# Seven block products in place of eight for the second product of a graph layer, with two re-ordered stretches

## The chip, the cores and the metric

The kernel runs on one core of a Trainium2 chip. The core has five engines, each of which works through its own instructions in order: TensorE (matrix products, "PE" in the profile, its weight loads are "PEld"), VectorE ("DVE"), ScalarE ("ACT"), GpSimd ("POOL") and SyncE ("SP", which issues transfers). They wait for one another through semaphores. SBUF is the on-chip memory, and PSUM the eight banks that TensorE writes its products to. The metric is the device time of one execution in microseconds (us), smaller is better.

All arithmetic is float32. A matmul instruction in float32 leaves two records in the trace, so "x16" beside a product means eight instructions.

## The reference, cut to what matters

Four graph layers, each added to its input (`x = x + layer(relu(layernorm(x)))`). The input has 128 x 64 x 256 elements, and the kernel works on it in 16 chunks of 512 tokens. The change touches layer 0 and the beginning of the last stretch, in which layers 2 and 3 run together.

```python
# layer 0 (h = relu(layernorm(x)), A_hat = normalised adjacency)
agg = einsum('nm,bmd->bnd', A_hat, h).reshape(-1, 256)
h1  = relu(batchnorm(agg @ W1.T + b1))      # 256 -> 512 channels, statistics over all 8192 tokens
out = batchnorm(h1 @ W2.T + b2)             # 512 -> 256 channels: "the second product"
# layer 2: attention with q, k, v and an output projection
# layer 3: attention with four heads; q and k by seven block products already
```

The batch normalisation needs all tokens before the first value can be used. So the first product runs for all chunks (keeping `z1`, 512 channels, in SBUF), then its statistics are put together, then the second product runs for all chunks.

## The kernel before

The second product of a chunk: four ReLU instructions on ScalarE write `h1`, eight matmuls (four channel blocks `k` for each of two output blocks `m`) fill two PSUM banks, and VectorE takes statistics and copies with the bias. The line numbers are those that the profile names.

```python
    def product2(chunks, by_block):
        h1 = {c: l0b.tile([P, KH, CH], F32, tag="h1", ...) for c in chunks}     # two buffers
        banks = {(c, m): bank(f"z2_{c}_{m}") for c in chunks for m in range(KD)}
        for k in range(KH):
            for c in chunks:
                nc.scalar.activation(h1[c][:, k, :], z1[c][k], AF.Relu, ...)             # L360
        ...
            nc.tensor.matmul(banks[c, m], w2_sb[:, k, ...], h1[c][:, k, :], ...)         # L364
        for c in chunks:
            for m in range(KD):
                nc.vector.bn_stats(st2[:, m, c, :], banks[c, m])                         # L368
                nc.vector.tensor_scalar(z2[c][:, m, :], banks[c, m], bn2_sb[...], ...)   # L369
    # [...]
    product2([0, 1], True)            # the first two chunks, block by block
    # [...]
        for c in range(2, NCH):       # NCH = 16
            if c == NCH - 2:
                weight_transposes()
            if wanted:
                weight_sums(*wanted.pop(0))     # 12 sets for layer 1: 2 loads, 4 GpSimd sums (L483), 2 stores
            product2([c], False)
        sc2, sh2 = bn_params(st2, bn2_sb, const, "bn2", False)
```

In this stretch only TensorE's order is given by hand (`manual_schedule(engines={PE})`); the order on the other engines comes out of the framework's scheduler when the kernel is built. `weight_sums` has two buffers, so a set's loads wait for the stores of the set before the last one.

The opening, by hand on all engines: adjacency, layer normalisation of chunk 0 in two halves (`a00`, `a01`), normalised adjacency, then chunk 1.

```python
        dinv = degrees(setup, others)
        keep_busy(34, "a")                                   # transposes that only keep TensorE at work
        stats = [ln_stats(xts[0], "a00", parts[0])]
        nc.vector.tensor_add(an, adj_bd, ident)
        normalized(setup, an, dinv)                          # rows, transpose (PE), ahat_t from PSUM
        keep_busy(10, "b")
        stats.append(ln_stats(xts[0], "a01", parts[1]))
        for i in range(2):
            ln_apply(hs[0], xts[0], *stats[i], f"a0{i}", parts[i])
        mv, rstd = ln_stats(xts[1], "a1")
        aggregate0(0)
        ln_apply(hs[1], xts[1], mv, rstd, "a1")
        keep_busy(8, "c")
```

Layers 2 and 3 are pipelined over the chunks: a round is a string of steps, `q2+0` being step `q2` for the round's chunk, `exp3-3` step `exp3` for the chunk three before. The first round (chunk 3) follows a filling sequence FIRST, and was the common round with its first two steps swapped:

```python
    FIRST = """... v3a+0 load3+1 v3b+0 apply3+2 square3+2"""          # end of the filling
        run(FIRST, 0)
        ring_places()                                                  # four GpSimd sums of weights (L1276)
        run(ROUND.replace("exp3-3 q2+0 copyq2+0", "q2+0 copyq2+0 exp3-3"), SUP + 1)
        for c in range(SUP + 2, NCH - SUP - 1):
            run(ROUND, c)
    # apply3: four ReLU on ScalarE (L174); square3: four transposes on VectorE (L259)
    # q2: a product on PE (L1108), half copied by ScalarE (L1169); copyq2: the other half by VectorE (L1174)
    # score2: products of q2 and the input (L1191)
```

Of the kernel before, what the change touches and what calls it, by code (L numbers as in the profile page):

```python
# [13 lines left out]
P = 128  # L14
# [5 lines left out]
def kernel(  # L20
# [65 lines left out]
    def bank(name, tag="ps"):  # L86
        return psum[0][0].tile([P, CH], F32, tag=tag, name=name, bufs=psum[0][1][tag])
# [39 lines left out]
    def normalized(setup, an, dinv):  # L127
        rows = setup.tile([P, P], F32, name="rows")
        nc.vector.tensor_scalar(rows, an, dinv, None, op0=OP.mult)
        pt = bank("pt_ahat")  # L130
        nc.tensor.transpose(pt[:, :P], rows, ident)
        nc.vector.tensor_scalar(ahat_t, pt[:, :P], dinv, None, op0=OP.mult)

# [20 lines left out]
    def ln_stats(src, name, tiles=range(NJ)):  # L154
        n = len(tiles)
        st = small.tile([P, n, 6], F32, tag=f"ln_st{n}", name=f"st_{name}")
        mv = small.tile([P, n, 2], F32, tag=f"ln_mv{n}", name=f"mv_{name}")
        for i, j in enumerate(tiles):
            nc.vector.bn_stats(st[:, i, :], src[:, j, :])
            nc.vector.bn_aggr(mv[:, i, :], st[:, i, :])  # L160
        rstd = small.tile([P, n], F32, tag=f"ln_rstd{n}", name=f"rstd_{name}")
        rsqrt(rstd, mv[:, :, 1], EPS)
        return mv, rstd

    def ln_apply(dst, src, mv, rstd, name, tiles=range(NJ), by_pool=False):
# [107 lines left out]
    def bn_params(stats, bn, pool, name, biased):  # L273
# [15 lines left out]
        return sc, sh  # L289


    GATES = (0, 2, 3, 1)
# [21 lines left out]

    z1, hs, aggs = {}, {}, {}

# [19 lines left out]
    def product1(c):  # L336
# [4 lines left out]
        for m in range(KH):  # L341
# [8 lines left out]
            nc.vector.bn_stats(st1[:, m, c, :], z1[c][m])  # L350
        z2[c] = lo

    def product2(chunks, by_block):
# [12 lines left out]
        for c in chunks:  # L366
            for m in range(KD):
                nc.vector.bn_stats(st2[:, m, c, :], banks[c, m])  # L368
                nc.vector.tensor_scalar(z2[c][:, m, :], banks[c, m], bn2_sb[:, 0, m : m + 1], None,  # L369
                                        op0=OP.add)  # L370

    with tc.manual_schedule(engines={mybir.EngineType.PE, mybir.EngineType.DVE,
# [18 lines left out]

        parts = [range(2 * i, 2 * i + 2) for i in range(2)]
        stats = [ln_stats(xts[0], "a00", parts[0])]
        an = setup.tile([P, P], F32, name="an")
        nc.vector.tensor_add(an, adj_bd, ident)
        normalized(setup, an, dinv)
        keep_busy(10, "b")
        stats.append(ln_stats(xts[0], "a01", parts[1]))  # L400
        for i in range(2):
            ln_apply(hs[0], xts[0], *stats[i], f"a0{i}", parts[i])
        mv, rstd = ln_stats(xts[1], "a1")
        aggregate0(0)
        ln_apply(hs[1], xts[1], mv, rstd, "a1")
        keep_busy(8, "c")
# [4 lines left out]
    with tc.manual_schedule(engines={mybir.EngineType.PE}):  # L411
# [4 lines left out]
        w2_sb = l0b.tile([P, KH, D], F32, name="w2_sb", bufs=1)  # L416
        nc.gpsimd.dma_start(w2_sb, w2t.rearrange("(k p) f -> p k f", p=P))
        for c in range(1, NCH):
            if c + 1 < NCH:
                aggregate0(c + 1)  # L420
            if c + 2 < NCH:
                norm0(c + 2)
            product1(c)
# [19 lines left out]

        def weight_transposes():
            for f in range(3 * KD):
                ps = bank(f"wt_{f}")
# [42 lines left out]
        wanted = [(p, q) for p in range(2, SKIP + 1) for q in GATES]  # L489
        for c in range(2, NCH):  # L490
            if c == NCH - 2:
                weight_transposes()
            if wanted:
                weight_sums(*wanted.pop(0))
            product2([c], False)
        sc2, sh2 = bn_params(st2, bn2_sb, const, "bn2", False)
        c2_ps = weight_products()
# [171 lines left out]
    BLOCKS = {1: (0, 8), 2: (2, 9), 3: (7, 14), 4: (3, 10), 5: (4, 11), 6: (5, 12), 7: (6, 13)}  # L669

    def differences(engine, dst, b11, b12, b21, b22):

        t1, t2, t3, t4 = dst
        return [lambda: engine.tensor_tensor(t1, b12, b11, OP.subtract),
                lambda: (engine.tensor_tensor(t3, b22, b12, OP.subtract),
                         engine.tensor_tensor(t2, b22, t1, OP.subtract)),
                lambda: engine.tensor_tensor(t4, b21, t2, OP.subtract)]

# [825 lines left out]
    def store(c, t):  # L1504
# [3 lines left out]
        for r in range(2):  # L1508
# [7 lines left out]
               v3a-2 qd-2 apply3+0 out3-3 score3-2 store-3 square3+0 v3b-2"""  # L1516

    NORM = """exp3-3 q2+0 copyq2+0 sum3-3 load3-1 sums_h-2 v2a+0 divide3-3 score2+0 exp2+0 v2b+0 norm2+1
              divide2+0 turn3-3 qa-2 turn2+0 q5-2 c11-2 out2+0 keep+0 norm3a+0 qb-2 apply2+1 back-2 qc-2
# [8 lines left out]
               norm3+1 pair1+15 pair1+15 q31+0 k31+0 apply3+1 out2+2 keep+2 square3+1 score3+0 norm3+2  # L1528
               v3a+0 load3+1 v3b+0 apply3+2 square3+2"""
    LAST = """exp3-2 sum3-2 load3+0 divide3-2 qa-1 q5-1 c11-1 v3a-1 qb-1 c12-1 qc-1 turn3-2 out3-2 qd-1  # L1530
# [10 lines left out]
    with tc.manual_schedule(engines={mybir.EngineType.PE, mybir.EngineType.DVE,  # L1541
# [6 lines left out]
        ring_places()  # L1548
        run(ROUND.replace("exp3-3 q2+0 copyq2+0", "q2+0 copyq2+0 exp3-3"), SUP + 1)
        for c in range(SUP + 2, NCH - SUP - 1):  # L1550
# [55 lines left out]
```

## Time and profile before

The median of three runs is 1924.26 us (1924.07 to 1924.88). The profile's span is cut here into stretches. Busy times are those of the answer that gives each engine's busy time in given stretches.

| stretch, us | what | PE busy | DVE | ACT | POOL |
|---|---|---|---|---|---|
| 0 to 25.5 | opening | 20.77 | 12.21 | 11.34 | 8.51 |
| 25.5 to 145.9 | layer 0, first product | 120.34 | 71.50 | 73.34 | 22.99 |
| 145.9 to 257.1 | layer 0, second product | 111.20 | 49.77 | 46.79 | 36.69 |
| 257.1 to 1560 | start of layer 1, layer 1 | 1295.65 | 773.34 | 668.61 | 240.42 |
| 1560 to 1588.8 | filling of layers 2 and 3 | 28.10 | 18.91 | 10.85 | 3.75 |
| 1588.8 to 1617.5 | first round | 25.60 | 16.86 | 11.91 | 10.61 |
| 1617.5 to 1924.8 | the other rounds, end | 300.23 | 215.78 | 135.54 | 90.04 |

How to read it: where PE is busy for the whole stretch, only fewer or shorter products help, provided that the other engines still keep up; where it is not, something else ends the wait. The granted clock of TensorE is given with each stretch: it is 1.00 in all of them but the opening (0.93) and the first round (0.88).

### The profile page before, as it was taken

Reading aid. Unit: us, or ns where it says so; the run is one execution under the profiler, and the core shown is the slowest. Engines: PE = TensorE matmul, PEld = TensorE weight load, DVE = VectorE, ACT = ScalarE, POOL = GpSimd, SP = SyncE. Lnnn points to the kernel's source line nnn. Section 1 sums busy time; section 2 is a strip of 40 time slices with the busy share of each in tenths; the row PEclk is TensorE's granted clock in tenths of the full one; section 3 lists DMA queues with packets and bytes.
Section 4 is the critical chain, followed back from the end, with each engine's and each line's share of the span. In section 5 each row is a group of like instructions: output and inputs, shape, how many; then the busy total and the mean of one; then the engine's idle time right before and its main releaser. Section 6 shows DMA issues by size and latency. Waiting matters only on the chain.

```text
span 1924.8 us, 38314 instructions
## 1 busy us (share of the span) xinstructions
PE 1901.9 (99%) x14979; PEld 1463.0 (76%) x14979; DVE 1158.4 (60%) x3019; ACT 958.4 (50%) x2132; POOL 413.0 (21%) x613
## 2 busy tenths in 40 slices
PE   9999999999999999999999999999999999999998
PEld 5444455897897889699689789879969967777776
DVE  6644354556557656755755665665555566677776
ACT  5655434445456455455545545545554543444453
POOL 3204210211211121121121121112112113233232
PEclk9999999999999999999999999999999999999999
DMA  4115711224524521532542452252144244445433
GB/s 130 64 42 211 279 60 66 83 83 160 159 83 141 186 97 64 174 105 93 189 141 83 159 181 83 96 190 103 56 150 128 90 143 142 134 133 154 143 111 111
DMA packets 110499, 240.35 MB, mean 125 GB/s; under 512 B 11376, under 2 KB 74352, under 8 KB 110320
## 3 DMA queue, kind: packets, MB, share of 16 engines
q1 hardware_dynamic: 109568, 236.57, 37.0%
q8 instruction: 118, 1.93, 0.4%
q0 software_dynamic: 320, 1.05, 0.2%
q14 instruction: 61, 0.50, 0.1%
q10 hardware_dynamic: 432, 0.30, 0.0%
HBM read 169.98 MB, written 67.90 MB: 124 GB/s over the span
## 4 chain that ended last, share of the span: by engine, by line
PE 94%; DVE 3%; ACT 1%; DMA 1%; issue 1%; POOL 0%; SPq 0%; DVEq 0%; ACTq 0%; POOLq 0%
PE x L829 22%; PE g L793 18%; PE z L829 11%; PE z L347 6%; PE y L829 6%; PE z L364 6%; PE v L1101 5%; PE p_q L1108 3%; PE u L574 3%; PE v L560 3%; PE X L1297 3%; PE Y L1297 1%; PE agg_a L201 1%; PE agg_c L201 1%; PE s L1191 1%; PE agg_b L201 1%
## 5 line engine op out<-in xcount | busy, mean ns | idle before, releaser
L838 DVE TENSOR_TENSOR gates<-gates,x 128x128 f32<-128x128 f32 (+2 forms) x384 | 119.4, 322 | 334.9 <-PE x L829 327.9
L829 PE MATMUL x<-xd,wset 128*128 128x128 f32 (+2 forms) x1280 | 285.2, 311 | 0.4 <-DVE gates L838 0.2
L829 PE MATMUL x<-hd,wset 128*128 128x128 f32 (+2 forms) x1152 | 246.7, 303 | 0.0
L829 PEld LDWEIGHTS x<-xd,wset 128*128 128x128 f32 x1280 | 202.1, 190 | 17.7 <-DVE gates L838 3.9
L887 POOL TENSOR_TENSOR gates<-gates 128x512 f32<-128x512 f32 (+2 forms) x48 | 74.9, 1559 | 648.1 <-ACT gates L721 648.1
L721 ACT ACTIVATE gates<-gates,bias 128x256 f32<-128x256 f32 (+4 forms) x384 | 170.4, 491 | 67.0 <-DVE gates L838 64.2
L829 PEld LDWEIGHTS x<-hd,wset 128*128 128x128 f32 x1152 | 185.1, 191 | 5.0
L772 ACT ACTIVATE gates<-g,bias 128x512 f32<-128x512 f32 (+2 forms) x240 | 138.0, 609 | 98.1 <-PE g L793 94.7
L793 PE MATMUL g<-hT,wset 128*128 128x256 f32 (+2 forms) x744 | 184.4, 405 | 1.1 <-DVE hT L732 1.1
L793 PEld LDWEIGHTS g<-hT,wset 128*128 128x128 f32 x744 | 140.5, 190 | 44.1 <-issue 8.8
L793 PE MATMUL g<-hT,wih 128*128 128x512 f32 x384 | 166.4, 592 | 0.0
L835 ACT COPY gates<-y 128x128 f32<-128x128 f32 (+2 forms) x192 | 54.1, 293 | 205.4 <-PE y L829 205.0
L829 PE MATMUL z<-hs,wset 128*128 128x128 f32 (+2 forms) x768 | 154.1, 303 | 0.0
L793 PEld LDWEIGHTS g<-hT,wih 128*128 128x128 f32 x384 | 72.3, 190 | 87.7 <-issue 83.2
L829 PEld LDWEIGHTS z<-hs,wset 128*128 128x128 f32 x768 | 119.8, 191 | 3.3
L347 PE MATMUL z<-agg,w_sb 128*128 128x512 f32 x256 | 114.5, 600 | 0.0
L778 DVE TENSOR_TENSOR cell<-gates 128x512 f32<-128x512 f32 (+2 forms) x80 | 50.3, 646 | 101.3 <-ACT gates L772 101.2
L364 PE MATMUL z<-h,w_sb 128*128 128x512 f32 x256 | 110.2, 592 | 0.0
L838 DVE TENSOR_TENSOR gates<-gates,z 128x128 f32<-128x128 f32 (+2 forms) x384 | 104.6, 316 | 0.1
L835 ACT COPY gates<-x 128x128 f32<-128x128 f32 (+2 forms) x192 | 56.5, 295 | 93.9 <-PE x L829 93.1
L721 ACT ACTIVATE gates<-x,bias 128x128 f32<-128x128 f32 (+2 forms) x192 | 74.7, 389 | 50.9 <-PE x L829 48.0
L829 PE MATMUL z<-hT,wset 128*128 128x128 f32 (+1 forms) x512 | 96.9, 301 | 0.0
(243 smaller groups left out, 3644.2 us busy)
## 6 DMA issues: line engine op xcount, KB each, us to landing
wset<-wfar SPq DMA_DIRECT2D x96, 960.0 KB, 6.4
hT<-far_h SPq DMA_DIRECT2D x124, 128.0 KB, 2.9
far_h<-hm SPq DMA_DIRECT2D x16, 512.0 KB, 3.8
far_n<-xs SPq DMA_DIRECT2D x16, 512.0 KB, 7.2
xs<-far_n SPq DMA_DIRECT2D x64, 128.0 KB, 3.1
far_x<-xs SPq DMA_DIRECT2D x16, 512.0 KB, 3.0
x<-far_x SPq DMA_DIRECT2D x64, 128.0 KB, 3.2
xt<-in_x_dram SPq DMA_DIRECT2D x15, 512.0 KB, 4.0
```

The lines of the kernel that those rows point to most:

```text
L201: nc.tensor.matmul(banks[e][half(i), k, j, :], src[half(e), j, f], mat[half(e), half(e)], start=True, stop=True)
L347: nc.tensor.matmul(ps, w1_sb[:, k, m * P : (m + 1) * P], agg[:, k, :], start=(k == 0), stop=(k == KD - 1))
L364: nc.tensor.matmul(banks[c, m], w2_sb[:, k, m * P : (m + 1) * P], h1[c][:, k, :], start=(k == 0), stop=(k == KH - 1))
L721: nc.scalar.activation(gate(q, c, part), src, AF.Tanh if q == 2 else AF.Sigmoid, bias=bs[:, q * KD + c : q * KD + c + 1])
L772: nc.scalar.activation(columns_of(gate(q, c)), natural(banks[q, c][:, :n].rearrange("p (w b) -> p w b", b=nb)), AF.Tanh if q == 2 else AF. ...
L793: nc.tensor.matmul(banks[q, c][:, :n].rearrange("p (w b) -> p w b", b=nb)[:, w, :], block(q, c, k), hv[:, k, w.start * p : (w.stop - 1) * ...
L829: nc.tensor.matmul(folded(self.psum(kind)), wsets[p, self.q][:, BLOCKS[kind][i], :], (ox[self.s] if part == "x" else oh)[kind], start=firs ...
L835: nc.scalar.copy(gate(self.q, kind // 5, halves[kind // 5]), self.psum(kind))
L838: nc.vector.tensor_add(gate(self.q, *dst), gate(self.q, *a), self.psum(kind))
L887: nc.gpsimd.tensor_mul(gates[:, 0, :, :n], gates[:, 0, :, :n], gates[:, 2, :, :n])
L1101: nc.tensor.matmul(ps[:, i, :], hT[:, k, j, :], w[:, k, first : first + D], start=(k == 0), stop=(k == KD - 1))
L1297: nc.tensor.matmul(st[c, tag][:, i * CH // 2 : (i + 1) * CH // 2].rearrange("p (a n) -> p a n", n=P), w, st[c, "o7"][kind], start=first an ...
```

## The change

Three parts.

1. For chunks 2 to 14 the second product is done by seven block products in place of eight (Winograd's form of Strassen's scheme). The 512 input channels are two blocks of rows, the 512 tokens two halves, the 256 output channels two blocks. Sums of weight blocks are made once on GpSimd, sums of data blocks on VectorE, and one of four (`t3`) on GpSimd. Seven products of 2 x (128 x 256) collect in three half-filled PSUM banks X, Y and Z; ScalarE copies four quarters, VectorE adds three. The ReLU is done in place in `z1`, and the result goes back into `z1` too. The products P7 and P4 of a chunk stand among those of the next one, so that TensorE has work while an add or a copy is under way.
2. The opening's order on VectorE is changed: the statistics of the second half of chunk 0 go between other steps, `ahat_t` is taken from PSUM later, and chunk 1's statistics are split in two.
3. The first round gets an order of its own (THIRD): `apply3` and `square3` of chunk 2 move from the end of FIRST to behind `copyq2` and `exp2`, `score2` to ahead of GpSimd's sums, and a `v3a` is brought forward.

The statistics of the second product are now taken from the copied values in SBUF (with the bias), not from PSUM.

```diff
-                nc.vector.bn_stats(st2[:, m, c, :], banks[c, m])
                 nc.vector.tensor_scalar(z2[c][:, m, :], banks[c, m], bn2_sb[...], None, op0=OP.add)
+                nc.vector.bn_stats(st2[:, m, c, :], z2[c][:, m, :])
+    def seven2(c):
+        for k in range(KH):
+            nc.scalar.activation(z1[c][k], z1[c][k], AF.Relu, ...)                # in place
+        b = {(k, j): a[:, :, halves[j]] for k, a in enumerate(z1whole[c]) for j in range(2)}
+        t = l0b.tile([P, 4, KH // 2, CH // 2], F32, tag="h1", name=f"t2_{c}")     # two buffers
+        for f in differences(nc.vector, t, ..., nc.gpsimd): f()     # t1, t2, t4 VectorE, t3 GpSimd
+        at = {1: b[0, 0], 2: b[1, 0], 3: b[1, 1], 4: t[3], 5: t[0], 6: t[1], 7: t[2]}
         # [...] product(kind, bank): two matmuls 128 x 256 that add to the bank
+        product(2, "Z")
+        yield
+        product(1, "X"); copy(0, 0, "X")
+        yield
+        product(5, "Y"); copy(1, 1, "Y"); add(0, 0, "Z")
+        yield
+        product(6, "X"); copy(0, 1, "X")
+        yield
+        product(3, "Y"); add(0, 1, "Y"); bn_stats(... 0 ...)
+        yield
+        product(7, "X"); add(1, 1, "X")
+        yield
+        product(4, "X"); copy(1, 0, "X"); bn_stats(... 1 ...)
+        yield
         # [...] opening
+        late = ln_moments(xts[0], "a01", parts[1])
+        next(late)
         nc.vector.tensor_add(an, adj_bd, ident)
-        normalized(setup, an, dinv)
-        keep_busy(10, "b")
-        stats.append(ln_stats(xts[0], "a01", parts[1]))
+        pt = normalized(setup, an, dinv)
+        keep_busy(12, "b")
+        next(late)
+        stats.append(next(late))
+        ln_apply(hs[0], xts[0], *stats[0], "a00", parts[0])
+        nc.vector.tensor_scalar(ahat_t, pt[:, :P], dinv, None, op0=OP.mult)
+        ln_apply(hs[0], xts[0], *stats[1], "a01", parts[1])
         # [...] the loop of the second product
-        for c in range(2, NCH):
+        last = iter(())
+        for c in range(2, NCH - 1):
             if wanted:
                 weight_sums(*wanted.pop(0))
-            product2([c], False)
+            kinds = seven2(c)
+            for turn in (kinds, last, kinds, kinds, last, kinds, kinds):
+                next(turn, None)
+            last = kinds
+        weight_transposes(range(2)); next(last)
+        weight_transposes(range(2, 3 * KD)); next(last)
+        product2([NCH - 1], False)
         # [...] layers 2 and 3
+    THIRD = """q2+0 copyq2+0 apply3-1 exp3-3 load2+1 v2a+0 score2+0 exp2+0 square3-1 sum3-3 load3-1 sums_h-2
+               v2b+0 divide3-3 divide2+0 qa-2 v3a-2 turn3-3 turn2+0 q5-2 c11-2 out2+0 keep+0 norm3a+0 qb-2
+               back-2 qc-2 norm3b+0 c12-2 qd-2 apply3+0 out3-3 score3-2 store-3 square3+0 v3b-2"""
-               v3a+0 load3+1 v3b+0 apply3+2 square3+2"""
+               v3a+0 load3+1 v3b+0"""
-        run(ROUND.replace("exp3-3 q2+0 copyq2+0", "q2+0 copyq2+0 exp3-3"), SUP + 1)
+        run(THIRD, SUP + 1)
```

In the order of TensorE, one chunk `c` of the new loop is thus P2(c), P7(c-1), P1(c), P5(c), P4(c-1), P6(c), P3(c).

## The prediction

> **What bounds the kernel now.** I read the page's chain first, then the chain in order of time, then the timeline of the three stretches that change.
>
> ```profile
> PE 94%; DVE 3%; ACT 1%; DMA 1%; issue 1%; POOL 0%; SPq 0%; DVEq 0%; ACTq 0%; POOLq 0%
> ```
>
> TensorE sets the end, so a stretch gains what TensorE loses there, in products or in waits. The chain in order of time gives the prices:
>
> ```profile
> 146.08 96.13 PE z L364 x224
> 243.53 13.73 PE z L364 x32
> ...
> 275.23 3.46 PE u L574 x16
> ```
>
> The second product is one unbroken run. 32 records (two chunks) take 13.73 us, so a chunk of 16 takes 6.87 us. Products of 128x256 (L574) take 3.46 / 16 = 0.216 us a record, so one block product of the new scheme (4 records) 0.866 us.
>
> The timeline of the second product's start, for the speed of the other engines:
>
> ```profile
> 149.77 0.16 DVE L287 TENSOR_TENSOR sh_bn<-mv_bn,sc_bn 128x1 f32<-128x1 f32 x1
> 153.05 0.65 DVE L287 TENSOR_TENSOR sh_bn<-mv_bn,sc_bn 128x1 f32<-128x1 f32 x1
> 154.41 1.52 ACT L360 ACTIVATE h<-z1b,sh_bn,sc_bn 128x512 f32<-128x512 f32 x2 [2.74 <-DVE sh_bn L288]
> 157.28 0.70 DVE L368 BATCH_NORM_STATS2 st<-z 128x6 f32<-128x512 f32 x1 [2.90 <-PE z L364]
> 158.20 1.52 ACT L360 ACTIVATE h<-z1a,sh_bn,sc_bn 128x512 f32<-128x512 f32 x2 [2.27 <-PE z L364]
> 159.62 1.50 ACT L360 ACTIVATE h<-z1b,sh_bn,sc_bn 128x512 f32<-128x512 f32 x2
> 161.03 1.50 ACT L360 ACTIVATE h<-z1a,sh_bn,sc_bn 128x512 f32<-128x512 f32 x2
> ```
>
> Unhindered pairs of ReLU start at 159.62 and 161.03: one ReLU per 0.705 us. And ScalarE is not free now: at 158.20 it had waited 2.27 us for TensorE, because `h1` has only two buffers.
>
> GpSimd's own timeline, its weight sums:
>
> ```profile
> 164.72 5.75 POOL L483 TENSOR_TENSOR ws<-ws 128x256 f32<-128x256 f32 x8 [6.70 <-DMA ws<-in_whh_t_dram]
> 176.72 5.75 POOL L483 TENSOR_TENSOR ws<-ws 128x256 f32<-128x256 f32 x8 [6.24 <-DMA ws<-in_whh_t_dram]
> ```
>
> A pair of sets costs 5.75 us of work every 12.0 us; the rest is waiting for loads.
>
> The first round of layers 2 and 3, TensorE's timeline and the granted clock (PEclk is the third column from the end, before DMA share and GB/s) in stretches of one microsecond:
>
> ```profile
> 1596.50 0.33 PE L1191 MATMUL s<-hT,q 128*64 128x64 f32 x2 [2.35 <-ACT q L1169]
> 1597.57 1.97 PE L1191 MATMUL s<-hT,q 128*64 128x64 f32 x30 [0.74 <-DVE q L1174]
> ...
> 1603.05 1.39 PE L1135 MATMUL tr<-ident,s 128*128 128x128 f32 x8
> ```
>
> ```profile
> 1595.00:1596.00 1.00, 0.00 (x0) 0.00 (x0) 0.48 (x2) 1.00 (x3) 1.00 (x3) 1.00 0.00 0
> 1596.00:1597.00 1.00, 0.33 (x2) 0.19 (x2) 1.00 (x4) 1.00 (x2) 1.00 (x2) 0.97 0.00 0
> 1599.00:1600.00 1.00, 1.00 (x11) 0.86 (x8) 1.00 (x1) 0.00 (x0) 0.00 (x0) 0.50 0.17 49
> 1603.00:1604.00 1.00, 1.00 (x7) 0.95 (x6) 0.32 (x1) 0.58 (x1) 0.00 (x0) 0.61 1.01 244
> 1604.00:1605.00 1.00, 1.00 (x9) 0.92 (x7) 0.00 (x0) 0.95 (x2) 0.00 (x0) 1.00 1.06 219
> ```
>
> TensorE waits 2.35 and 0.74 us for two copies of `q2` that stand behind `apply3` and `square3`, and then pays twice: its clock is 0.50 until about 1603.6.
>
> The opening:
>
> ```profile
> 10.66 0.13 DVE L172 SCALAR_TENSOR_TENSOR nmr_a<-mv_a,rstd_a 128x2 f32<-128x2 f32 x1
> 12.07 1.09 ACT L174 ACTIVATE h<-xt,nmr_a,rstd_a 128x256 f32<-128x256 f32 x2 [0.16 <-DVE nmr_a L172]
> ```
>
> **What the Trainium skill says.** "TensorE: Matmul & The Clock Gate", Part 1, What's actually happening: TensorE's clock falls to half after an idle window of some 3.4 us and returns after about as long a busy one. The trace agrees: 0.50 after 3.1 us of idling in 3.4 us, for some 6.6 us. "SBUF — State Buffer", Who interferes with whom: a VectorE instruction with two SBUF inputs and a GpSimd instruction that reads SBUF exclude each other, one waits for the whole of the other. The trace agrees: the same 128x1 product took 0.16 us at 149.77 and 0.65 us at 153.05, when GpSimd's sums of 0.72 us each were running. The new `t1`, `t2`, `t4` have two SBUF inputs; the adds from PSUM and the statistics don't.
>
> **Part 1, the second product.** *Work.* Seven products: 7 x 0.866 = 6.06 us a chunk in place of 6.87. For 13 chunks that is 13 x 0.81 = 10.5 us less on TensorE, if nothing makes it wait. Per chunk the other engines have, of 6.06 us: ScalarE 4 x 0.705 plus four copies of 128x256 at about 0.37 (such a copy, L465, took 0.37 us) = 4.3; VectorE three differences at 0.65 (128x512 from SBUF, L778, 0.646 mean on the page), two statistics at 0.65, three adds of 128x256 at 0.4 = 4.4; GpSimd 2.88 of weight sums plus `t3` at 1.27 (L887 took 1265 ns for 128x512) = 4.15. All fit on the average. The order decides.
>
> *Order on ScalarE.* I read it from the order of the changed kernel's instructions on each engine. In place, a ReLU needs no free buffer, and so the scheduler has put ReLUs of chunks 2 to 6 ahead of the first copy. After the last two ReLUs of chunks 0 and 1 (154.41 to 155.82, as now) come 18 ReLUs, and only then the copy of P1(2): 155.82 + 18 x 0.705 = 168.5, done near 168.95. TensorE ends the eight blocks of chunks 0 and 1 at 145.92 + 13.73 = 159.66. P2(2) and P1(2) follow to 161.39. P5(2) needs `t1`, which on VectorE stands behind seven evictions and statistics of 0.62 each from 157.28 and meets GpSimd's `t3`: about 162.9, a wait of 1.5 us. It ends at 163.8. P6(2) adds to the bank that the copy has to read first: it waits to 169.0, 5.2 us. Waits together 6.7 us.
>
> *Clock.* A gap of 5.2 us after one product within 2.4 us is worse than the one in the first round, so I expect the clock at half after it, with a loss near 3.3 us (6.6 us at half). I give this 70%: 2.3 us.
>
> *Later waits.* ScalarE has by then done the ReLUs to chunk 6, and works through the rest among the copies; TensorE waits there little. Two sources remain. GpSimd's order has `t3` of chunk 10 behind the eleventh set of weight sums; those are paced by loads, and walking the queue with 9.15 us from a set's end to its buffer's next sums puts `t3`(10) near 220.4 to 221.7, its dependent copy of Y at 222.1, and P3(10), due at about 220.4, 1.8 us late. In the same way chunks 7 and 9 lose about 0.5 each. VectorE's differences meet GpSimd in the port, which delays the last add before P4 by 0.1 to 0.6 in several chunks, together about 1.5. Together 4.3; without the port's effect 0.2. I take 3.2.
>
> *Sum:* -10.5 + 6.7 + 2.3 + 3.2 = +1.7 us. The stage comes out about even, although the product is an eighth shorter.
>
> **Part 2, the opening.** The first half's statistics are ready on GpSimd at 9.46, but VectorE reaches their use (L172) at 10.66, having waited for `ahat_t` and done two tiles of statistics. Now it comes before `ahat_t`, one 0.6 us tile having gone ahead of `rows`: near 9.8. ScalarE starts the first half at about 9.95 (10.83 before), the second at 11.15 (12.07). The chain goes through them to the first product, which is 0.9 us earlier, and TensorE is busy from there on. -0.9.
>
> **Part 3, the first round.** From the start of `q2`(3) at 1588.82 to that of `q2`(4) at 1617.53 are 28.7 us; the following rounds take 22.33. So 6.4 us can be had: 3.1 of waits and 3.3 of clock. In the new order the copies are done at 1591.2 and 1593.1, before `v2a` ends at 1594.0, and `score2` follows at once. Left: `divide3`(0) behind `square3` and the sum on VectorE, which delays `turn3`(0) by about 0.85; `turn2`(3) by 0.2; and P4 directly behind P7 in this round, 0.8 for the add between. 1.85 us of waits in three places, none long enough for the clock. -6.4 + 1.85 = -4.6.
>
> **Sum:** 1924.3 + 1.7 - 0.9 - 4.6 = 1920.5 us.
>
> **Rivals.** (a) The seven products pay in full: ScalarE's copy is not late, because the built order doesn't act as I read it. Then 1924.3 - 10.5 + 1 to 3 - 5.5 = 1910 or so. For it: all busy sums fit into 6.06 us. Against: eighteen ReLUs without a wait between them and no buffer to hold them back. I give it 12%. (b) The port between VectorE and GpSimd, or GpSimd's loads, become the bound of the whole stage: 2.0 + 4.15 us of exclusive use a chunk make 6.15 against 6.06. Each chunk then loses some 0.5 us more, 13 x 0.5 = 6 us: 1925. For it: the sum; against: GpSimd's sums end with chunk 12 or so. 12%. (c) The gain of the first round is given back, as its chunk is ahead of transfers: 1925. Against it: the transfers it needs (`load2`, `load3`) are issued earlier too. 5%.
>
> **Range and chances.** The two clear gains make -5.5, give or take 1; the second product lies between -4 (no port effect, no clock loss) and +5. Eight in ten: 1914.5 to 1924.5. Two per cent are 38 us, far from anything here: within 2% almost certain.
>
> **What would show it.** Right: a wait of TensorE of about 5 us at P6 of chunk 2, near 164, released by ScalarE's copy; PEclk 0.50 after it; the chunks from 11 on at 6.06 us; layer 1 starting within 3 us of before; `score2`(3) without a wait and a first round near 24 us; the first product 0.9 us earlier. Wrong: chunks of 6.06 us from the start (rival a), or all chunks at 6.5 with waits for VectorE and GpSimd (rival b); a first round still above 26 us.

## The result, and the profile after

| kernel | us, median | lowest to highest | runs |
|---|---|---|---|
| before | 1924.16 | 1923.86 to 1924.88 | 4 |
| changed | 1928.14 | 1926.58 to 1929.15 | 4 |

The ratio is 1.0016, with a 95% interval of 1.0001 to 1.0031: a loss of 0.2 to 6 us. I had predicted 1920.5 and a range that ends at 1924.5.

The same views, now of the changed kernel. TensorE's timeline at the start of the second product (start, duration, in brackets the idle time before and its releaser):

```profile
158.44 1.03 PE L421 MATMUL X<-z1a,w_sb 128*128 128x256 f32 x4
160.87 1.10 PE L421 MATMUL Y<-t,w_sums 128*128 128x256 f32 x4 [1.40 <-DVE t L308]
167.06 2.05 PE L421 MATMUL X<-t,w_sums 128*128 128x256 f32 x4 [5.08 <-ACT z1a L425]
168.89 1.91 PE L421 MATMUL Y<-z1b,w_sums 128*128 128x256 f32 x4
170.60 1.89 PE L421 MATMUL Z<-z1b,w_sb 128*128 128x256 f32 x4
172.31 1.05 PE L421 MATMUL X<-t,w_sums 128*128 128x256 f32 x4
```

P6 of chunk 2 (167.06) waits 5.08 us for ScalarE's copy. Then P6, P3 and P2 take 5.25 us from 167.06 to 172.31, where three block products at full speed take 2.6. The stretches of one microsecond say why: the third column from the end, the granted clock, is 0.50.

```profile
164.00:165.00 1.00, 0.00 (x0) 0.00 (x0) 0.00 (x0) 1.00 (x2) 0.92 (x2) 1.00 0.00 0
167.00:168.00 1.00, 0.94 (x2) 0.84 (x3) 1.00 (x2) 1.00 (x3) 0.92 (x3) 0.50 1.02 410
171.00:172.00 1.00, 1.00 (x4) 0.79 (x3) 1.00 (x3) 1.00 (x3) 0.00 (x0) 0.50 1.03 376
173.00:174.00 1.00, 1.00 (x6) 0.90 (x5) 0.42 (x1) 0.00 (x0) 0.00 (x0) 1.00 0.97 330
```

ScalarE's timeline shows the row of in-place ReLUs, without a gap, and the copy at its end:

```profile
154.49 1.51 ACT L400 ACTIVATE z1b<-z1b,sh_bn,sc_bn 128x512 f32<-128x512 f32 x2
...
165.78 0.81 ACT L400 ACTIVATE z1b<-z1b,sh_bn,sc_bn 128x512 f32<-128x512 f32 x1
166.49 0.47 ACT L425 ACTIVATE z1a<-X,bn_sb 128x256 f32<-128x256 f32 x1
```

So far this is the prediction, in its places and nearly in its numbers. What follows isn't. TensorE's timeline later in the stage:

```profile
202.16 1.13 PE L421 MATMUL Y<-z1b,w_sums 128*128 128x256 f32 x4 [0.66 <-ACT z1a L425]
...
216.74 2.08 PE L421 MATMUL Y<-z1b,w_sums 128*128 128x256 f32 x4 [2.23 <-ACT z1a L425]
218.61 1.78 PE L421 MATMUL Z<-z1b,w_sb 128*128 128x256 f32 x4
220.23 1.03 PE L421 MATMUL X<-t,w_sums 128*128 128x256 f32 x4
...
226.45 1.13 PE L421 MATMUL Y<-z1b,w_sums 128*128 128x256 f32 x4 [1.74 <-ACT z1a L425]
...
232.60 1.03 PE L421 MATMUL Y<-z1b,w_sums 128*128 128x256 f32 x4
```

Each is P3 of a chunk (7, 9, 10). The second wait starts another stretch at half clock: P3 and P2 take 3.49 us instead of 1.73. The last line and its successor at 238.64 are one undisturbed chunk apart: 6.04 us, the full worth of seven products. "<-ACT" is only the last link. ScalarE's and GpSimd's timelines show the one before:

```profile
216.21 0.47 ACT L425 ACTIVATE z1a<-Y,bn_sb 128x256 f32<-128x256 f32 x1 [3.73 <-POOL t L309]
...
225.92 0.47 ACT L425 ACTIVATE z1a<-Y,bn_sb 128x256 f32<-128x256 f32 x1 [3.24 <-POOL t L309]
```

```profile
207.50 7.46 POOL L579 TENSOR_TENSOR ws<-ws 128x256 f32<-128x256 f32 x8 [4.23 <-DMA ws<-in_whh_t_dram]
214.92 1.26 POOL L309 TENSOR_TENSOR t<-z1b,z1a 128x512 f32<-128x512 f32 x1
221.31 2.91 POOL L579 TENSOR_TENSOR ws<-ws 128x256 f32<-128x256 f32 x4 [5.13 <-DMA ws<-in_whh_t_dram]
224.18 1.71 POOL L309 TENSOR_TENSOR t<-z1b,z1a 128x512 f32<-128x512 f32 x1
```

GpSimd waits 4.23 us for the loads of a set, adds up two sets (7.46 us), and only then computes `t3` of chunk 9 (214.92). The copy of Y writes over an operand of `t3` (`z2` lies in `z1a`), so it waits for `t3`, and P3, which adds to the bank that the copy reads, waits for the copy.

The first round of layers 2 and 3 on TensorE. The start of `q2`(3) at 1594.66 and of `q2`(4) at 1618.22 are 23.56 us apart (28.71 before), `score2` (1599.91) doesn't wait, and one wait is left:

```profile
1594.66 3.60 PE L1204 MATMUL p_q<-hT,wqk_sb 128*128 128x512 f32 x8
1598.10 1.89 PE L1197 MATMUL v<-wvo_sb,hT 128*128 128x256 f32 x8
1599.91 1.20 PE L1287 MATMUL s<-hT,q 128*64 128x64 f32 x32
...
1613.33 1.10 PE L1393 MATMUL X<-td,w_sb 128*128 128x256 f32 x4 [0.94 <-DVE qk L1432]
```

The balance of the two profiles, along TensorE:

| from, to | before | changed | difference |
|---|---|---|---|
| start to the first product | 15.62 | 13.49 | -2.13 |
| first product | 130.30 | 130.36 | +0.06 |
| second product, to the first product after it (`c`) | 111.18 | 117.94 | +6.76 |
| to `q2`(3) | 1331.72 | 1332.87 | +1.15 |
| to `q2`(4) | 28.71 | 23.56 | -5.15 |
| to the end of the span | 307.27 | 308.58 | +1.31 |
| sum | 1924.8 | 1926.8 | +2.0 |

The +1.15 is at the start of layer 1, where waits of the same length as before now give a half clock (`v` in 4.76 us instead of 3.67). The change isn't shown to be its cause: ring_only, whose layers 0 and 1 are those of before, has a half clock there too, from 268.48 to 271.89. The last +1.31 lies behind the last instruction: 4.4 us from the issue of the last store to the end, 3.1 before. The profiled run of before was 2.6 us above the median of before, which is why the medians differ by 4.0 and the profiles by 2.0.

### The profile page after: what moved, and what is told of

It is laid out like the page before. It is cut to its first block, busy times and chain, and to the rows that moved or that the text cites. A ratio compares the mean times of both kernels' runs of the same rounds, so it can differ in the third digit from the quotient of the medians.

```text
span 1926.8 us, 38815 instructions
## 1 busy us (share of the span) xinstructions
PE 1895.2 (98%) x15137; PEld 1493.2 (77%) x15137; DVE 1188.3 (62%) x3070; ACT 981.7 (51%) x2184; POOL 443.9 (23%) x632
## 3 DMA queue, kind: packets, MB, share of 16 engines
q0 software_dynamic: 320, 1.05, 0.2%
## 4 chain that ended last, share of the span: by engine, by line
PE 91%; DVE 3%; ACT 1%; DMA 1%; POOL 1%; issue 1%; SPq 0%; DVEq 0%; POOLq 0%; ACTq 0%
PE x L925 22%; PE g L889 18%; PE z L925 11%; PE y L925 6%; PE v L1197 5%; PE z L369 5%; PE p_q L1204 3%; PE u L678 3%; PE v L664 3%; PE X L1393 3%; PE X L421 1%; PE Y L1393 1%; PE z L386 1%; PE agg_c L214 1%; PE o L1318 1%; PE agg_b L214 1%
## 5 line engine op out<-in xcount | busy, mean ns | idle before, releaser
L369 PEld LDWEIGHTS z<-agg,w_sb 128*128 128x128 f32 x256 | 47.3, 190 | 54.6 <-issue 51.2
```

What stands on the lines that cost most here:

```text
L369: nc.tensor.matmul(ps, w1_sb[:, k, m * P : (m + 1) * P], agg[:, k, :], start=(k == 0), stop=(k == KD - 1))
```

## The experiments

The times of before were taken beside each group on the same chip: 1926.1 us in the first and third, 1926.0 in the second, where single runs lie between 1922.6 and 1929.1. Read ratios, not times across groups. "Stage" is the second product as in the table above (111.18 before, 117.94 changed).

### The three parts alone

**ring_only**: before, with the order `THIRD` and the shortened `FIRST` and nothing else.

```diff
-        run(ROUND.replace("exp3-3 q2+0 copyq2+0", "q2+0 copyq2+0 exp3-3"), SUP + 1)
+        run(THIRD, SUP + 1)
```

> The kernel before with part 3 alone (the new order of the first round). My theory: the whole of the 5.15 us by which that round is shorter in the changed kernel's trace (23.56 in place of 28.71) arrives at the end: 5 us less than before, to within 1. Rival: the round only moves ahead of its transfers and the rounds after it give it back, so less than 2 us remain.

1921.74 us, ratio 0.9979 (0.9971 to 0.9987): 2.5 to 5.6 us less. The round's 5.15 us arrive at the end or nearly so. The rival, that it is given back, falls. How much there is to gain differs from execution to execution: the old round took 28.71 us in the profile of before, with a half clock for 6.8 us, and 27.14 in that of opening_only, with 3.4 us of it; the new one took 23.55 in this run's.

**opening_only**: before, with the changed opening.

```diff
+        late = ln_moments(xts[0], "a01", parts[1])
+        next(late)
         ...
+        ln_apply(hs[0], xts[0], *stats[0], "a00", parts[0])
+        nc.vector.tensor_scalar(ahat_t, pt[:, :P], dinv, None, op0=OP.mult)
```

> The kernel before with part 2 alone (the opening). Theory A: the order is worth what I predicted, 0.9 us, and the rest of the 2.07 us between the two profiles is a half-clock spell that the profiled execution of before happened to have: 0.9 us less than before in the timed runs. Theory B: the spell belongs to the old order, so all of it is gained: 2 us less.

1923.61 us, ratio 0.9987 (0.9981 to 0.9994): 1.2 to 3.7 us less, more than my 0.9. The profiles tell why. Of the three profiled runs with the old opening (before, ring_only, seven_only), two have a half clock from 13 to 16 us and begin the first product at 15.62 and 15.86; ring_only's has none and begins it at 14.73. Of eleven profiled runs with the new opening none has it, and they begin at 13.49 to 14.40. So the order gives about 0.8 us (14.73 in ring_only against 13.92 in this run; it is one pair, and the new openings alone differ by 0.9), and the clock spell, another 0.9 to 1.1, is gone. Theory B is nearer.

**seven_only**: before, with the second product in seven block products.

```diff
-            product2([c], False)
+            kinds = seven2(c)
+            for turn in (kinds, last, kinds, kinds, last, kinds, kinds):
+                next(turn, None)
+            last = kinds
```

> The kernel before with part 1 alone (the second product in seven block products). My theory: the waits and half-clock spells of the second product's stage cost 6.8 us net and the new spell at the start of layer 1 some 1.4 more: 7 to 9 us slower than before. The prediction's size was 1.7 us slower. Rival: the stage's loss is made by the earlier start from the opening (its loads and sums come relatively later), so that without part 2 it is under 4 us.

1935.89 us, ratio 1.0055 (1.0043 to 1.0068): 8 to 13 us slower. Its stage took 117.47 us, +6.3, and TensorE waited at the same instructions (1.36 at P5 and 5.07 at P6 of chunk 2, then 0.22, 1.55 and 3.32 at P3 of chunks 7, 9 and 10), so the rival (the opening shifts the loads) falls. The rest is partly a cost that I had not looked for, ahead of the stage. While GpSimd computes the new `w2_sums` (25.2 to 28.1 us), two instructions of VectorE for the masks take 1.32 us together where one took 0.27 before, the normalisation of chunk 3 begins at 29.13 instead of 27.32, and TensorE waits once in the first product:

```profile
34.15 1.94 PE L201 MATMUL agg_a<-ahat_t,h 64*64 64x64 f32 x64 [1.32 <-ACT h L174]
```

The first product took 131.87 us, 1.6 more than before. In the changed kernel, where the masks come ahead of these sums, the same wait was 0.24. The three parts alone add up to -4.0 - 2.5 + 10.6 = +4.1 us by the ratios (of 1926), and the changed kernel has +3.1 by its ratio, +4.0 by its medians. The intervals would hide an interplay of some 3 us; the one that the traces show is the wait just named, which only seven_only pays in full.

### ScalarE's order: the wait at P6 goes, and the time grows

**relu_spread**: a chunk's ReLUs behind the third copy of the chunk before, by hand.

```diff
+    with tc.manual_schedule(engines={mybir.EngineType.PE, mybir.EngineType.Activation}):
         copy(0, 1, "X")
+        relu2(c + 1, (0, 1))
+        if c + 2 < NCH:
+            relu2(c + 2, (2, 3))
```

> The changed kernel with ScalarE's order in the second product fixed: a chunk's in-place ReLUs stand two by two behind the third copy of the chunk before, so no copy waits behind later chunks' ReLUs. My theory: the 5.08 us wait at P6 of chunk 2 goes, and with it the half-clock spell after it (2.7 us): 7 to 8 us less than the changed kernel, about 1920.5; the waits at P3 of chunks 7, 9 and 10 stay, as they come from t3 on GpSimd. Rival: VectorE's and GpSimd's sharing of SBUF binds the stage, and what is won at chunk 2 is lost in small waits of the chunks after it: less than 3 us.

1936.36 us, ratio 1.0055 (1.0043 to 1.0068). Neither the theory's number nor the rival's holds: the wait at P6 of chunk 2 and its spell are gone, and the stage took 125.5 us, 7.5 more than in the changed kernel. TensorE's timeline of this run:

```profile
187.30 1.13 PE L424 MATMUL Y<-z1b,w_sums 128*128 128x256 f32 x4 [2.88 <-ACT z1a L428]
204.90 1.47 PE L424 MATMUL Y<-z1b,w_sums 128*128 128x256 f32 x4 [3.55 <-ACT z1a L428]
227.59 1.13 PE L424 MATMUL Y<-z1b,w_sums 128*128 128x256 f32 x4 [2.61 <-ACT z1a L428]
245.08 2.08 PE L424 MATMUL Y<-z1b,w_sums 128*128 128x256 f32 x4 [4.46 <-ACT z1a L428]
```

and GpSimd's, from the start of the stage to the first of them:

```profile
166.67 1.27 POOL L309 TENSOR_TENSOR t<-z1b,z1a 128x512 f32<-128x512 f32 x1 [7.82 <-ACT z1a L397]
167.91 7.97 POOL L587 TENSOR_TENSOR ws<-ws 128x256 f32<-128x256 f32 x8
...
182.13 3.40 POOL L587 TENSOR_TENSOR ws<-ws 128x256 f32<-128x256 f32 x4 [4.58 <-DMA ws<-in_whh_t_dram]
185.48 1.26 POOL L309 TENSOR_TENSOR t<-z1b,z1a 128x512 f32<-128x512 f32 x1
```

Four times `t3` stands behind a set of sums that waits for its loads. But more than the ReLUs has moved: with ScalarE's order by hand, the scheduler put `t3` of chunks 2 and 3 ahead of the first set of sums, which so began at 167.91 and not at 150.20. The next run, as_changed_fixed_order, is therefore the proper comparison. It has the changed kernel's row of early ReLUs, by hand, and the same two `t3` ahead of the first set (at 159.62), and its stage took 123.9 us. Of the 7.5 us, then, 6.0 came with the hand-written order and only 1.5 with spreading the ReLUs. The times of the two can't be told apart (ratios 1.0055 and 1.0046, with overlapping intervals). What is shown is that the wait at P6 can go without a shorter stage, and that `t3` behind the sums makes the waits that remain.

**as_changed_fixed_order** and **wait_filled**: the changed kernel with ScalarE's order written out by hand, and the same with TensorE kept busy in its wait.

```diff
+        if c == 2:
+            keep_busy(38, "z")
         product(6, "X")
```

> Control for the next run: the changed kernel with ScalarE's order of the second product written out by hand as the scheduler had it (19 ReLUs of chunks 2 to 6, then the first copy). Expected like the changed kernel: a wait of 5.1 us at P6 of chunk 2, then P6, P3 and P2 at 1.7 to 1.9 us instead of 0.87; small differences in GpSimd's order may move the later waits by 1 to 3 us.

> The control with 38 transposes (some 4.5 us) of a constant put before P6 of chunk 2, which do nothing but keep TensorE busy in its wait. My theory: the wait and the half clock are two costs; P6 still starts when the copy is done, near 167, but P6, P3 and P2 then take 0.87 each: 2.7 us less than the control. Rival: the slow products come from the operands' side (VectorE, ScalarE and GpSimd all writing SBUF at that moment), not from the clock: no difference.

The control took 1934.56 us, ratio 1.0046 (1.0033 to 1.0060), not the time of the changed kernel: with ScalarE by hand the scheduler put GpSimd's instructions in another order, and P3 waited 2.02, 3.20 and 3.42 us; its wait at P6 was 3.70. The pair still tells wait and clock apart, since up to that point GpSimd's order is the same in both. TensorE in the control, then in the filled run:

```profile
166.53 2.05 PE L427 MATMUL X<-t,w_sums 128*128 128x256 f32 x4 [3.70 <-ACT z1a L432]
168.37 1.64 PE L427 MATMUL Y<-z1b,w_sums 128*128 128x256 f32 x4
```

```profile
162.83 4.31 PE L151 MATMUL idle_z<-ident 128*128 128x128 f32 x38
166.98 1.03 PE L427 MATMUL X<-t,w_sums 128*128 128x256 f32 x4
167.85 1.03 PE L427 MATMUL Y<-z1b,w_sums 128*128 128x256 f32 x4
```

P6 begins nearly at the same moment (0.45 us later), and P6 to P2 then take 2.59 us in place of 4.19. The slow products come from the clock; with the operands written at nearly the same moments they are fast. The total didn't follow (1935.29, ratio 1.0047, 1.0034 to 1.0061): P3 waited 4.97, 3.71 and 3.71 us, and the stage took 127.6 us. From its third set on, GpSimd's order is another one again (`t3` of chunk 4 ahead of the fourth set), so whether the time saved was waited away at the late `t3`s or lost by that order, this pair doesn't show.

### Taking t3 out of the queue of the sums

**t3_on_vector**: the changed kernel, `t3` on VectorE.

```diff
-        for f in differences(nc.vector, t, b[0, 0], b[0, 1], b[1, 0], b[1, 1], nc.gpsimd):
+        for f in differences(nc.vector, t, b[0, 0], b[0, 1], b[1, 0], b[1, 1]):
```

> The changed kernel with t3 computed on VectorE instead of GpSimd. My theory: the waits at P3 of chunks 7, 9 and 10 (0.66, 2.23, 1.74) and the half-clock spell after the second go, since t3 no longer stands behind weight sums that wait for loads; the 5.1 us wait at P6 of chunk 2 stays: 4 to 6 us less than the changed kernel. Rival: with four differences, 5.05 us of work a chunk and the sums of GpSimd on the same SBUF port, VectorE becomes the bound of the chunks up to 12 or so (6.5 us each): no gain or a loss of up to 4 us.

1922.45 us, ratio 0.9985 (0.9977 to 0.9993); the stage took 109.66 us, 8.3 less than in the changed kernel. After chunk 2 no wait of TensorE is left in it, and no half clock. This one line turns the loss into a gain (6 us less than the changed kernel by the ratios, the upper end of what was expected), and the rival (VectorE becomes the bound) falls. The wait at P6 stays, with 5.34 us.

**spread_and_vector**: the edits of relu_spread and of t3_on_vector together.

```diff
+        relu2(c + 1, (0, 1))          # as in relu_spread
-        for f in differences(nc.vector, t, b[0, 0], b[0, 1], b[1, 0], b[1, 1], nc.gpsimd):
+        for f in differences(nc.vector, t, b[0, 0], b[0, 1], b[1, 0], b[1, 1]):
```

> ReLUs spread as in relu_spread, and t3 on VectorE. My theory: relu_spread lost because late ReLUs put t3 behind a set of weight sums (waits of 2.6 to 4.5 us at P3 of chunks 4, 5, 7, 10, 13); without GpSimd on the path neither the 5.1 us wait nor those are left: 10 us less than relu_spread and about as far below the kernel before (1914). Rival: the four differences come late in turn, since they can't start before their ReLUs, and TensorE waits for VectorE at P5 or P4 in each chunk, 0.3 to 0.5 us: 1920 or more.

1924.77 us, ratio 0.9995 (0.9987 to 1.0003), stage 113.3 us, 3.6 more than in t3_on_vector: the rival holds, with longer waits in fewer chunks than it said. The differences, now just in time too, delay VectorE's additions, and P4 waits about 1.05 us in five chunks:

```profile
178.68 1.13 PE L424 MATMUL X<-t,w_sb 128*128 128x256 f32 x4 [1.05 <-DVE z1a L432]
```

**t3_first**: `t3` stays on GpSimd, but a chunk's differences are written one chunk ahead and ahead of a set of sums, with GpSimd's order by hand.

```diff
-            for turn in (kinds, last, kinds, kinds, last, kinds, kinds):
-                next(turn, None)
+            for turn in (kinds, last, kinds, kinds, last, None, kinds, kinds):
+                if turn:
+                    next(turn, None)
+                elif c + 1 < NCH - 1:
+                    prepare2(c + 1)          # ReLUs and differences of the next chunk
+            if wanted:
+                weight_sums(*wanted.pop(0))
```

> The changed kernel with GpSimd's order fixed: the differences of a chunk are written one chunk ahead, and t3 stands before the set of weight sums whose loads are latest. ScalarE's order is still the scheduler's; with this emission nine ReLUs in place of eighteen stand before the first copy. My theory: the waits at P3 go, and the wait at P6 of chunk 2 shrinks from 5.1 to about 2 us: 9 us less than the changed kernel. Rival: the weight sums start later and in step with the chunks, so the same port conflicts and loads hit every chunk, and the waits only move to other chunks: within 3 us of the changed kernel.

The stage took 104.82 us, 13.1 less than in the changed kernel, with one wait of 2.09 us at P5 of chunk 2 and two below 0.3. And yet 1926.67 us, ratio 1.0002 (0.9993 to 1.0010): the rival's number, but not at the rival's place. The gain is lost right behind the stage, at layer 1's first aggregation. SyncE's issues, VectorE's and TensorE's timelines:

```profile
246.22 3.44 SPq L643 DMA_DIRECT2D wset<-wfar  x6
249.86 2.42 SPq L705 DMA_DIRECT2D early<-in_x_dram  x2
266.52 0.69 DVE L716 TENSOR_TENSOR xs<-early,at_b 128x512 f32<-128x512 f32 x1 [12.53 <-DMA early<-in_x_dram]
271.01 2.39 PE L214 MATMUL agg_b<-adjt_bd,cv 64*64 64x64 f32 x64 [12.20 <-ACT cv L187]
```

The sums end later in this order (the last set was stored at 241.6, in the changed kernel at 229.1), so the six loads of weight sets, 5.8 MB, are issued late, and the loads of `x` that layer 1 needs first stand behind them. They landed 16.8 us after their issue (median of the two).

A variant of it with the ReLUs spread (**t3_first_spread**) took 1934.05 us, ratio 1.0043 (1.0029 to 1.0057).

```diff
+                elif c + 1 < NCH - 1:
+                    prepare2(c + 1)          # as in t3_first, differences only
         copy(0, 1, "X")
+        relu2(c + 1, (0, 1))                 # as in relu_spread
```

> ReLUs spread as in relu_spread together with GpSimd's order of t3_first. My theory: neither the wait at P6 of chunk 2 nor those at P3 are left; P5 of chunk 2 still waits 1.5 us: 10 us less than the changed kernel and 16 less than relu_spread, near 1914. Rival: with ReLUs only one chunk ahead t3 can't be early, GpSimd's sets of sums still stand before it, and the loss of relu_spread stays (over 1925).

By a slip in it half of a chunk's ReLUs came after its differences, so the kernel leaves out the ReLU in some of their operands, and its order isn't the one meant. I read nothing from its time.

**x_first**: t3_first with `x` loaded ahead of the weight sets.

```diff
-    load_sets(6)
         ...
             next(convs[i])            # the first two of these issue the loads of x
+            if n == 1:
+                load_sets(6)
```

> t3_first with the two loads of x for layer 1 issued before the six loads of weight sets instead of after them. My theory: t3_first had won the second product's waits (its stage ended 4.7 us before that of t3_on_vector) and lost 12.20 us at layer 1's first aggregation, only because those loads stood in one queue behind 5.8 MB of weight sets that had themselves become late; with the order turned, that wait and the half clock after it go: 12 to 14 us less than t3_first, near 1913. Rival: the weight sets, which are now last, are missing in turn when layer 1's second step starts, and the 12 us only move there: no less than 1922.

1915.60 us, ratio 0.9945 (0.9931 to 0.9958): 8 to 13 us below before, some 11 below t3_first (12 to 14 expected), and the best version of the study. The two loads are issued first, land 6.4 us after it, and the aggregation waits only as long as it did before the change:

```profile
246.36 0.92 SPq L704 DMA_DIRECT2D early<-in_x_dram  x2
247.32 3.77 SPq L643 DMA_DIRECT2D wset<-wfar  x6
```

```profile
260.68 0.95 PE L214 MATMUL agg_b<-adjt_bd,cv 64*64 64x64 f32 x32 [1.09 <-ACT cv L187]
```

The rival falls: from the end of the stage to `q2`(3) this kernel takes 1331.51 us and the kernel before 1331.72, so layer 1 doesn't miss the sets.

**x_first_t1_early**: x_first with the evictions of chunks 0 and 1 written behind `t1` of chunk 2.

```diff
-        product2([0, 1], True)
+        begun = product2([0, 1], True)       # now stops ahead of its evictions
+        next(begun)
         ...
         prepare2(2)
+        next(begun)
```

> x_first with the evictions of chunks 0 and 1 written behind the differences of chunk 2, so that t1 of chunk 2 stands three instructions earlier on VectorE. Theory: the wait at P5 of chunk 2 (2.09 us in t3_first) shrinks by the 1.9 us of three instructions: 1.5 to 2 us less than x_first. Rival: t1 then only waits for its ReLUs or for GpSimd on the shared port: no difference.

1917.23 us, ratio 0.9952 (0.9940 to 0.9965): no gain. The wait at P5 of chunk 2 is gone, as the theory has it, but waits at P3 of 0.46, 1.55 and 2.04 us have come in its place, behind `t3` and sets that wait up to 4.5 us for loads; the stage took 107.4 us, 2.5 more than in x_first. Neither expectation held: the wait named in the theory went, and others took its place.

## Why the prediction was wrong

**The work of seven products, -10.5: right.** 6.04 us a chunk, wherever nothing waits.

**The first chunk's waits, 6.7 us: right.** 1.40 + 5.08 = 6.48, at the instructions named and with the releasers named. **The clock after them, 2.3: right in kind.** The figure was 70% of a loss of 3.3; the loss came, with 2.66, as 1.5 us of the spell of 6.8 passed while TensorE still waited. wait_filled showed that it is the clock.

**The later waits, 3.2 us: wrong, and this is the step that failed.** The stage lost 6.76 + 10.5 = 17.3 us against its work; without 6.48 and 2.66, 8.1 us are left for this term. The mechanism was in the prediction: `t3` behind sets of sums paced by loads. What failed is the walk along GpSimd's queue, which I had made with the durations of before: 2.88 us a set, and 9.15 us from a set's end to its buffer's next sums. The additions before and now:

```profile
L483 POOL TENSOR_TENSOR ws<-ws 128x256 f32<-128x256 f32 x48 | 33.6, 727 | 33.9 <-DMA ws<-in_whh_t_dram 33.0
L579 POOL TENSOR_TENSOR ws<-ws 128x256 f32<-128x256 f32 x48 | 39.9, 856 | 15.2 <-DMA ws<-in_whh_t_dram 14.3
```

I had looked at the shared port only as a delay for VectorE; GpSimd pays as well. The Trainium skill says so ("SBUF — State Buffer", Who interferes with whom: a VectorE instruction with two SBUF inputs and a GpSimd instruction that reads SBUF contend, and the order of issue decides which of them waits), and the trace agrees: of the 48 additions, 33 took 0.72 to 0.75 us and 15 took 1.04 to 1.25, and each of these 15 ran beside one of VectorE's new differences. A pair of sets took 5.75 us before and up to 7.46 now, and `t3` 1.26 us alone and 1.7 beside the differences.

The second figure grew too. From a set's end to its buffer's next sums the trace has 9.0 to 12.6 us, and 10.5 and 11.3 for the two sets ahead of `t3` of chunk 9. On SyncE a set's loads stand behind the stores of the set before it, so a set that takes longer can hold back the next loads (the stores of the fifth had landed by 185.37, but the loads of the seventh, which need its buffer, were issued at 187.82, right behind the stores of the sixth at 187.29). So P3 of chunk 9 waited 2.23 where I had 0.5, and that was enough for a second stretch at half clock (1.76 us), which the sum did not have at all. 4.63 us of waits at P3 and this clock make 6.4 of the 8.1; the rest is in small delays of 0.03 to 0.3, some of them the start after each wait. P3 of chunk 10 did wait 1.74 (1.8 predicted), but that is luck: its `t3` ran from 224.18 to 225.89, where I had 220.4 to 221.7, and TensorE came as much later. That the whole term hangs on `t3`'s place is shown by t3_on_vector: its stage is 8.3 us shorter.

How much of the lateness is the slower additions and how much the later loads was not tried apart. In t3_on_vector the additions were slower still (907 ns) and nobody waited for them.

**The opening, -0.9: the mechanism right, the size short.** ScalarE began the two halves at 9.77 and 11.02 (9.95 and 11.15 predicted). The gain is 2.13 us between the profiles, 1.2 to 3.7 timed. The missing term is the half-clock spell that two of the three profiles of the old opening have.

**The first round, -4.6: right.** 5.15 in the trace, 2.5 to 5.6 timed; the predicted wait of 0.8 for the addition between P7 and P4 measured 0.94.

**Missing from the sum:** the half clock at layer 1's start, about 1.1 us. The instructions and waits there are those of before, and it comes and goes: ring_only has it, x_first doesn't.

**The rivals.** (a), seven products that pay in full: not as built, though x_first comes nearer, its stage 6.3 us below that of before. (b), the whole stage bound by port or loads, 1925: near in the number, half right in the mechanism. The loads and the slowed sums did decide, but by three late `t3`s and not by every chunk; VectorE was not the bound. (c) is out by ring_only.

The range was too narrow for the same reason: it let the second product lie between -4 and +5, as if a queue on GpSimd could only delay TensorE by what it was late itself. A wait like that of 2.23 us could bring the clock's share on top, and I had allowed for that once. The profile of before held the sign: the prediction counts 3.1 us of idling ahead of the half clock of the first round, but the clock fell at 1596.94, when the second wait there (0.74, from 1596.83) had hardly begun, so the one of 2.35 us had been enough. It also reads the spell of some 6.6 us as in line with a busy window of 3.4; it was two steps of 3.4 us (1596.94 to 1603.77; the last section has these steps), and TensorE was busy for 0.81 of the first.

## What to carry to other kernels

When a small instruction on the critical path (`t3`) shares an in-order queue with work that waits for transfers, walk that queue with the durations that the change itself will cause, and put the small instruction ahead of the transfers' users or on another engine. A buffer that holds work back can also keep an order right: freed from it, a scheduler ran eighteen ReLUs ahead of the first copy. But the longest wait needn't be the one to attack: undoing just that row didn't shorten the stage, and with `t3` on VectorE it made it 3.6 us longer. When one engine's order is written by hand and the others' is left to a scheduler, look at what the others do now before reading the time: here that alone cost 6.0 us of the stage. And after each gain look at what is now issued later: t3_first's 13 us were lost again until two loads changed places with six.

## What the runs showed of the hardware that I had not expected

The length of a wait alone doesn't decide whether the clock falls. The wait of 2.23 us before 216.74 in the changed kernel was followed by 0.50 from 217 to 220; one of 2.61 in relu_spread (before 227.59) left it at 1.00, and one of 2.88 there (before 187.30) gave the half clock only from 188.49 on. The Trainium skill ("TensorE: Matmul & The Clock Gate", Part 1, What's actually happening) speaks of an idle window of some 3.4 us that runs freely, so that the moment of a change depends on where in the window the work falls.

The traces agree, and show where the windows lie. Within each trace all changes of the granted clock are whole steps of 3.413 us apart, to within 0.02 us: the half clocks of the changed kernel run from 165.52 to 172.34, from 216.72 to 220.13 and from 274.74 to 278.16, which is two steps, one and one. How busy TensorE was in such a step, from its busy time in that stretch:

| run | step, us | TensorE busy | clock in the next step |
|---|---|---|---|
| changed | 213.30 to 216.72 (wait of 2.23) | 0.35 | 0.50 |
| changed | 223.54 to 226.96 (wait of 1.74) | 0.49 | 1.00 |
| relu_spread | 185.07 to 188.49 (wait of 2.88) | 0.35 | 0.50 |
| relu_spread | 222.62 to 226.03 (first part of 2.61) | 0.69 | 1.00 |
| relu_spread | 226.03 to 229.44 (the rest of it) | 0.54 | 1.00 |

So a window need not be wholly idle. Over the second product's stage in all fourteen traces, the clock was halved behind 17 steps, with TensorE busy for 0 to 0.43 of each, and behind none with 0.48 or more; one step with 0.42 kept the full clock. The share isn't the whole account: at the start of layer 1, where the products are smaller, a step with 0.64 was followed by a half clock in the changed kernel, and one with 0.60 was not in the kernel before.
